# One-head layer: one score operation from two table columns, denominators of dense tiles on TensorE, dense means on ScalarE

## The chip, the core and the metric

The kernel runs on one core of one Trainium2 chip. The metric is the device time of one execution in microseconds (us), the median of several runs. The engines are TensorE (PE in the profile, its weight loads PEld), VectorE (DVE), ScalarE (ACT), GpSimd (POOL) and SyncE (SP), which here only issues transfers.

## What is computed

The reference is a stack of four graph attention layers on 3327 nodes with 512 features, all fp32. The adjacency is sparse (about 0.5% of its entries, the diagonal included). The layers have 8, 4, 1 and 8 heads. The change touches the third one alone, the layer with one head:

```python
h = features @ W
s1 = h @ attn[:512, 0]
s2 = h @ attn[512:, 0]
e = jax.nn.leaky_relu(s1[:, None] + s2[None, :], negative_slope=0.2)
e = jnp.where(adjacency > 0, e, -9e15)
h_prime = jax.nn.softmax(e, axis=1) @ h
return jax.nn.elu(h_prime)
```

Around it, as around every layer: `h = max(layernorm(x), 0)`, then `x = x + layer(h)`.

## The kernel before

**Tiles and order.** The nodes are ranked by their number of neighbours and cut into 26 tiles of 128 targets. For most tiles the neighbours' rows are gathered from a table in device memory by GpSimd's indirect transfers (`gather`, L835), one neighbour slot of all 128 targets at a time. In the one-head layer tiles 9 to 25 are done this way, and tiles 0 to 8, which have the most neighbours, are done densely over all 26 source blocks, with masks.

**The table.** A row has 528 columns: 256 features, 8 columns for scores, 256 features, 8 columns for scores. The score columns come out of the projection for free, because the products of the weights with the attention vectors are appended to the weights (class `Weights`, `fold`). In the one-head layer only the first of each 8 is used: column 256 holds a node's score as a target, column 520 (`ROW - 8`) its score as a source. The others are zero. One extra row, for empty slots, holds -30000 in all of the last 8 columns.

**Gathered tiles** (class `Tile`). The neighbours of a tile are taken in groups of up to four slots; a group is a step of the schedule, and the 17 tiles make 72 steps. `scored` copies the tile's own score once (L886), adds it to the neighbours' scores (L888), applies the slope 0.2 with a maximum (L890), and lets ScalarE take the exponential (L891). `group` accumulates weight times feature row on VectorE (L910, L912). When a tile is complete, `divisors` and `means` divide (L930 to L938), and `ends` places the rest: ELU, the addition to x, the next layer's normalization, transposes (L451), projection (L469) and the store of the next table (L996).

**Dense tiles** (class `Wholes`). They come in three groups of three tiles (384 targets). For each source block j, ScalarE computes r (`weights`, L1128), VectorE adds and masks it (`masked`, L1135, the tile em), and TensorE multiplies em with the block's feature rows into three banks, one for each tile (`products`, L1162). The denominators are column sums of em. GpSimd adds two blocks (`paired`, L1148), VectorE reduces two such pair sums and the sum so far (`added`, L1154), and at the end of the group TensorE sums over the partitions (`divisors`, L1169). VectorE then takes the reciprocal (L1173) and multiplies the three banks by it (`Whole.means`, L1089).

**Who goes when.** The order on VectorE, ScalarE, GpSimd and TensorE is written out by hand. A loop runs over the steps s and emits for each one: the gathers of step s + 4, the pieces hung at (s, "first"), the scores of step s + 1, the pieces at (s, "scored"), the accumulation of step s, and the pieces at (s, "last"). `later(s, place, piece)` hangs a piece in. Each engine then works through its own list in order. Dense block j of group p is masked at step 21p + floor(19j/26). Its products are emitted one step later, ahead of that step's mask product. The pair sum comes one step after its second block.

**Buffers.** The pool "o" holds one PSUM bank for the accumulator of a gathered tile and one for r. The pool "w" has three banks for the products, "t" has one for transposes, and the projection uses two. Gathered groups have five buffers, em has three pairs, and feature blocks of the dense part have four.

Of the kernel before, what the change touches and what calls it, by code (L numbers as in the profile page):

```python
# [10 lines left out]
F32 = mybir.dt.float32  # L11
# [4 lines left out]
OP = mybir.AluOpType  # L16
# [364 lines left out]
class Weights:  # L381
# [31 lines left out]

def centred(nc, xt, small, work):
# [382 lines left out]
def tile_gat_lists(ctx: ExitStack, tc: tile.TileContext, x, adj, ws, avs, out, ident, half, slots, L, low, spare, tabx, tabs):  # L797
# [48 lines left out]
    class Tile:  # L846
# [29 lines left out]
        def scored(self, i):  # L876

            H = HEADS[self.l]
            t = self.t
            k0, n, g = self.groups[i]  # L880
            if i == 0:
                self.po = pools["o"].tile([P, BANK], F32, name="bank")
                pw = next(scores)
                K = CAPS[t]
                self.wt, self.s = pw[:, :K * 8].rearrange("p (k h) -> p k h", h=8), pw[:, K * 8:K * 8 + H]
                nc.vector.tensor_copy(self.s, g[:, n, F:F + H] if self.l == 0 else g[:, 0, F // 2:F // 2 + H])  # L886
            z = small.tile([P, GROUP, 8], F32, name="z")[:, :n, :H]
            nc.vector.tensor_tensor(z, g[:, :n, ROW - 8:ROW - 8 + H],  # L888
                                    self.s.unsqueeze(1).to_broadcast([P, n, H]), OP.add)
# [37 lines left out]
        def divisors(self):  # L927
            H, K = HEADS[self.l], CAPS[self.t]
            den = self.den = small.tile([P, 8], F32, name="den")
            nc.vector.tensor_reduce(den[:, :H], self.wt[:, :K, :H].rearrange("p k h -> p h k"), AX.X, OP.add)  # L930
            nc.vector.tensor_scalar_max(den[:, :H], den[:, :H], TINY)
            nc.vector.reciprocal(den[:, :H], den[:, :H])
# [151 lines left out]
    class Whole(Tile):  # L1084


        def means(self):
            self.y = low[:, self.t % 3 * F:(self.t % 3 + 1) * F]
            nc.vector.tensor_scalar(self.y, self.po, self.den, None, OP.mult)  # L1089

    class Wholes:


        def __init__(self, l, W):
            self.l, self.tiles = l, [Whole(l, t, W) for t in range(ND)]
            self.s = pools["e"].tile([P, ND], F32, name="s", bufs=1)
            for t in range(ND):
                nc.sync.dma_start(self.s[:, t:t + 1], tabs[l % 2][t * P:(t + 1) * P, F // 2:F // 2 + 1])
            self.b, self.c, self.mc = [pools["e"].tile([P, NT], F32, name=n, bufs=1) for n in ("b", "c", "mc")]

            self.a = [low[:, 5 * F + p % 2 * wide:5 * F + (p % 2 + 1) * wide] for p in range(ND // 3)]
            self.v, self.e, self.mk, self.r, self.pairs, self.parts = {}, {}, {}, {}, {}, {}

        def targets(self, p):

# [12 lines left out]
        def weights(self, p, j):  # L1118
            if p == ND // 3:
                return  # L1120
            b, c, mc = [t[:, j:j + 1] for t in (self.b, self.c, self.mc)]
            if p == 0:
                d = self.v[p, j][:, ROW - 8:ROW - 7]
                nc.scalar.activation(b, d, AF.Exp)
                nc.scalar.activation(c, d, AF.Exp, scale=SLOPE)
                nc.scalar.activation(mc, c, AF.Copy, scale=-1.0)
            r = self.r[p, j] = pools["o"].tile([P, wide], F32, name="r")
            nc.scalar.activation(r, self.a[p], AF.Relu, scale=b, bias=mc)  # L1128

        def masked(self, p, j):  # L1130

            if j % 2 == 0:
                self.two = pools["e"].tile([P, 2, wide], F32, name="em", bufs=3)
            self.e[p, j] = self.two[:, j % 2, :]
            nc.vector.scalar_tensor_tensor(self.e[p, j], self.r.pop((p, j)), self.c[:, j:j + 1],  # L1135
                                           self.mk.pop((p, j)), OP.add, OP.mult)
            if j % 2:
                self.pairs[p, j // 2] = self.two

        def part(self, p, i):  # L1140
            if (p, i) not in self.parts:
                self.parts[p, i] = pools["e"].tile([P, 3, wide], F32, name="parts", bufs=2)
            return self.parts[p, i]

        def paired(self, p, i):

            two = self.pairs.pop((p, i))
            nc.gpsimd.tensor_tensor(self.part(p, i // 2)[:, 1 + i % 2, :], two[:, 0, :], two[:, 1, :], OP.add)  # L1148

        def added(self, p, i):  # L1150

            parts = self.part(p, i // 2)[:, i < 2:2 + i % 2, :]
            out_ = self.a[p] if i == NT // 2 - 1 else self.part(p, i // 2 + 1)[:, 0, :]
            nc.vector.tensor_reduce(out_, parts.rearrange("p j c -> p c j"), AX.X, OP.add)  # L1154

        def products(self, p, j):
            e, v = self.e.pop((p, j)), self.v.pop((p, j))
# [8 lines left out]
        def divisors(self, p):  # L1166
            self.pd = pools["t"].tile([P, F // P, P], F32, name="pt")
            for q in range(3):
                nc.tensor.matmul(self.pd[:, 0, q:q + 1], self.a[p][:, q * P:(q + 1) * P], one, start=True, stop=True)  # L1169
# [311 lines left out]
```

## Time and profile before

| | us |
|---|---|
| median of 3 runs | 2940.11 (2933.88 to 2944.69) |
| the profiled execution, its own time | 2959.5 |
| span of the profile | 2957.8 |
| busy in the span: TensorE | 2224.7 (75%) |
| VectorE | 1914.3 (65%) |
| GpSimd | 1728.5 (58%) |
| ScalarE | 931.8 (32%) |

A row of a group in the profile gives line, engine, operation, written and read tiles, shapes, count, then the busy time in us and the mean of one in ns, then the idle time of the engine just before it and what ended it. A row of waits gives total us, times, and the longest. "issue" means that the engine waited for nothing that the profile shows. A row of the timeline begins with the start and the duration in us; the bracket at its end is the idle time before it. One fp32 matmul shows as two instructions. Names ending in q are queues.

### The profile page before, as it was taken

The page shows a single profiled execution, that of the slowest core. Times are in us where ns is not written, and L with a number is a line of the kernel's source. Part 1 is how long each engine was busy: PE and PEld are TensorE (multiplying, and loading weights), DVE is VectorE, ACT ScalarE, POOL GpSimd, SP SyncE. Part 2 cuts the span into 40 slices and gives each one's busy share as a digit, 9 for nine tenths or more (in the row PEclk, how much of TensorE's full clock was granted, in tenths as well). Part 3 has the DMA queues.
Part 4 walks back from the last instruction along what each step waited for, and adds up shares of the span by engine and source line. Part 5 has one row for each costly group of instructions (what it writes and reads, how often), then busy time and mean ns, then how long its engine had stood idle before and what let it go on. Part 6 is the DMA issues. An engine that isn't in the chain of part 4 may idle for free.

```text
span 2957.8 us, 27080 instructions
## 1 busy us (share of the span) xinstructions
PE 2224.7 (75%) x7082; PEld 1251.4 (42%) x7082; DVE 1914.3 (65%) x4968; ACT 931.8 (32%) x2502; POOL 1728.5 (58%) x1717
## 2 busy tenths in 40 slices
PE   4777677787677745788877787689696778877887
PEld 2664243343333323344434344245354445444453
DVE  7887656565546523767765565698887556666665
ACT  5882122222221101323332222344333333333330
POOL 7894465565556663555655552676764555555554
PEclk9988788888888877899988889799897889988898
DMA  6885477677666675666766663788775666666664
GB/s 229 322 294 160 140 218 216 193 235 222 188 205 195 189 194 170 181 202 192 209 193 189 192 192 111 226 264 257 236 248 152 191 177 184 185 182 194 185 187 137
DMA packets 260730, 594.20 MB, mean 201 GB/s; under 512 B 103699, under 2 KB 121107, under 8 KB 256214
## 3 DMA queue, kind: packets, MB, share of 16 engines
q0 software_dynamic: 124368, 432.13, 49.8%
q1 hardware_dynamic: 132454, 153.45, 16.5%
q10 hardware_dynamic: 3744, 6.82, 0.7%
q8 instruction: 57, 0.93, 0.1%
q14 instruction: 107, 0.88, 0.1%
HBM read 542.60 MB, written 49.65 MB: 200 GB/s over the span
## 4 chain that ended last, share of the span: by engine, by line
DVE 21%; PE 18%; issue 16%; another core or an unknown queue 11%; ACT 6%; POOL 4%; DMA 3%; DVEq 0%; ACTq 0%; POOLq 0%; SPq 0%
PE bank L924 11%; DVE m L919 9%; POOL g L835 3%; PE pv L469 3%; PE whole L1310 3%; DVE bank L912 2%; DMA g<-tab,idxb 1%; DVE z L890 1%; DVE z L888 1%; ACT r L1276 1%; DVE x L962 1%; DVE q L439 1%; ACT pw L891 1%; DVE room L1292 1%
## 5 line engine op out<-in xcount | busy, mean ns | idle before, releaser
L924 PE MATMUL bank<-m,ident 128*128 128x512 f32 x2414 | 1236.5, 659 | 268.9 <-DVE m L919 137.5
L835 POOL DMA_INDIRECT g<-tab,idxb x712 | 678.2, 952 | 465.5 <-issue 189.3
L919 DVE TENSOR_TENSOR m<-g,pw 128x512 f32<-128x512 f32 x1207 | 752.0, 682 | 267.6 <-ACT pw L891 193.5
L924 PEld LDWEIGHTS bank<-m,ident 128*128 128x128 f32 x2414 | 490.2, 211 | 879.8 <-issue 568.9
L469 PE MATMUL pv<-w,hT 128*128 128x264 f32 x1664 | 447.4, 423 | 107.0 <-ACT hT L458 71.2
L835 POOL DMA_INDIRECT g<-tabx,twiceb x342 | 324.1, 948 | 245.8 <-issue 124.4
L835 POOL DMA_INDIRECT g<-tab,idxa x297 | 283.1, 953 | 262.1 <-DMA tab<-v 88.5
L469 PEld LDWEIGHTS pv<-w,hT 128*128 128x128 f32 x1664 | 339.5, 208 | 215.2 <-ACT hT L458 79.6
L891 ACT ACTIVATE pw<-z 128x32 f32<-128x32 f32 (+4 forms) x356 | 67.8, 190 | 945.4 <-DVE z L890 509.8
L1162 PE MATMUL whole<-ve,em 128*128 128x512 f32 x468 | 224.5, 632 | 48.2 <-DVE em L1135 27.9
L1310 PE MATMUL whole<-L,room 128*128 128x130 f32 x1248 | 171.1, 288 | 79.2 <-issue 79.0
L1310 PEld LDWEIGHTS whole<-L,room 128*128 128x128 f32 x1248 | 163.1, 201 | 107.1 <-issue 104.7
L695 POOL TENSOR_TENSOR key<-a,keys 128x3328 int32<-128x3328 int32 (+1 forms) x29 | 189.5, 6539 | 15.9 <-DVE cand L704 12.6
L912 DVE SCALAR_TENSOR_TENSOR bank<-g,L,bank 128x512 f32<-128x512 f32 x243 | 183.3, 754 | 9.9 <-remote 2.0
L835 POOL DMA_INDIRECT g<-tabx,twicea x99 | 94.4, 954 | 119.6 <-issue 75.3
L1162 PEld LDWEIGHTS whole<-ve,em 128*128 128x128 f32 x468 | 92.8, 203 | 158.7 <-issue 114.6
L451 PE MATMUL pt<-ident,xn 128*128 128x128 f32 x416 | 74.5, 302 | 93.0 <-issue 32.2
L704 DVE MAX8 cand<-key 128x8 f32<-128x208 int32 x416 | 143.6, 363 | 0.1
L890 DVE SCALAR_TENSOR_TENSOR z<-z 128x32 f32<-128x32 f32 (+5 forms) x428 | 82.5, 193 | 91.4 <-remote 61.4
L919 DVE TENSOR_TENSOR bank<-g,pw 128x512 f32<-128x512 f32 x74 | 51.5, 696 | 126.7 <-ACT pw L891 105.6
L1276 ACT ACTIVATE r<-low,L 128x384 f32<-128x384 f32 x208 | 121.2, 582 | 9.8 <-remote 3.9
L888 DVE TENSOR_TENSOR z<-g,pw 128x32 f32<-128x32 f32 (+4 forms) x356 | 61.8, 174 | 94.9 <-DMA g<-tab,idxa 39.0
(181 smaller groups left out, 2154.4 us busy)
## 6 DMA issues: line engine op xcount, KB each, us to landing
a<-in_adj SPq DMA_DIRECT2D x25, 1664.0 KB
tab<-v SPq DMA_DIRECT2D x78, 264.0 KB
ve<-tab SPq DMA_DIRECT2D x78, 264.0 KB
g<-tab SPq DMA_DIRECT2D x65, 264.0 KB
tabx<-vx SPq DMA_DIRECT2D x26, 528.0 KB
g<-tab,idxb POOLq DMA_INDIRECT x712
low<-tab SPq DMA_DIRECT2D x52, 132.0 KB
spare<-tab SPq DMA_DIRECT2D x52, 132.0 KB
```

The lines of the kernel that those rows point to most:

```text
L469: nc.tensor.matmul(pv[:, s, :HF + 8], hT[:, k, :], W.w[:, k, s, :], start=(k == 0), stop=(k == KC - 1))
L695: nc.gpsimd.tensor_tensor(key[:, c:c + quarter], a[:, c:c + quarter], keys[:, c:c + quarter], OP.mult)
L704: nc.vector.max(cand[:, g * 8:(g + 1) * 8], key[:, g * SEG:(g + 1) * SEG])
L835: nc.gpsimd.indirect_dma_start(out=out_, out_offset=None, in_=table, in_offset=bass.IndirectOffsetOnAxis(ap=which, axis=0))
L890: nc.vector.scalar_tensor_tensor(z, z, SLOPE, z, OP.mult, OP.max)
L891: nc.scalar.activation(self.wt[:, k0:k0 + n, :H], z, AF.Exp)
L912: nc.vector.scalar_tensor_tensor(acc, v, w, acc, OP.mult, OP.add)
L919: nc.vector.tensor_tensor(out_.rearrange("p (s h d) -> p s h d", s=2, d=D), v.rearrange("p s (h d) -> p s h d", d=D), wt[:, k0 + q, :H].re ...
L924: nc.tensor.matmul(self.po, ident, m[:, q, :], start=False, stop=(k0 + q == K - 1), skip_group_check=True)
L1162: nc.tensor.matmul(tl.po.rearrange("p (s m) -> p s m", s=2), e[:, q * P:(q + 1) * P], v.rearrange("p (s m) -> p s m", s=2)[:, :, :F // 2], ...
L1276: nc.scalar.activation(self.r[:, h, :], self.a[:, g, :], AF.Relu, bias=-1.0, scale=self.b[:, j, g:g + 1])
L1310: nc.tensor.matmul(dst, e[:, h, q * P:(q + 1) * P], mov, start=False, stop=(j == NT - 1), skip_group_check=True)
```

## The change

It has three parts, all in the one-head layer. First, the appended weight columns hold a second column each: the first one times 0.8 for the target's score, and times 0.2 for the source's. The table then holds 0.8 of a node's target score in column 257 and 0.2 of its source score in column 521. With s the target's and d the source's score, the step takes max(d + 0.8s, 0.2d) in one VectorE operation, and ScalarE copies 0.8s once for a tile. Second, each pair sum goes straight to TensorE, which adds its column sums to three columns for each group of tiles (`added`). These columns lie in the same PSUM bank as r, which is now one fixed tile. The step of `added` is s + 3, "first", for every pair; `divisors` and the partial sums are gone. Third, the means of dense tiles are ScalarE copies with a scale. Nothing changes in the transfers.

```diff
@@ Weights.fold
+        if self.H == 1:
+            nc.vector.tensor_scalar(self.w[:, k, s, HF + 1:HF + 2], self.w[:, k, s, HF:HF + 1],
+                                    SLOPE if s else 1.0 - SLOPE, None, OP.mult)
@@ Tile.scored
-                nc.vector.tensor_copy(self.s, g[:, n, F:F + H] if self.l == 0 else g[:, 0, F // 2:F // 2 + H])
+                if H == 1:
+                    nc.scalar.activation(self.s, g[:, 0, F // 2 + 1:F // 2 + 2], AF.Copy)
+                else:
+                    nc.vector.tensor_copy(self.s, g[:, n, F:F + H] if self.l == 0 else g[:, 0, F // 2:F // 2 + H])
             z = small.tile([P, GROUP, 8], F32, name="z")[:, :n, :H]
+            if H == 1:
+                nc.vector.scalar_tensor_tensor(z, g[:, :n, ROW - 8:ROW - 7], self.s, g[:, :n, ROW - 7:ROW - 6],
+                                               OP.add, OP.max)
+                nc.scalar.activation(self.wt[:, k0:k0 + n, :H], z, AF.Exp)
+                return
@@ Whole.means
-            nc.vector.tensor_scalar(self.y, self.po, self.den, None, OP.mult)
+            nc.scalar.activation(self.y, self.po, AF.Copy, scale=self.den)
@@ Wholes.__init__
+            bank = pools["o"].tile([P, BANK], F32, name="r")
+            self.r, self.pd = bank[:, :wide], [bank[:, wide + 8 * p:wide + 8 * p + 3] for p in range(ND // 3)]
@@ Wholes.weights
-            r = self.r[p, j] = pools["o"].tile([P, wide], F32, name="r")
-            nc.scalar.activation(r, self.a[p], AF.Relu, scale=b, bias=mc)
+            nc.scalar.activation(self.r, self.a[p], AF.Relu, scale=b, bias=mc)
@@ Wholes.paired
-            nc.gpsimd.tensor_tensor(self.part(p, i // 2)[:, 1 + i % 2, :], two[:, 0, :], two[:, 1, :], OP.add)
+            self.sums[p, i] = pools["e"].tile([P, wide], F32, name="sums", bufs=3)
+            nc.gpsimd.tensor_tensor(self.sums[p, i], two[:, 0, :], two[:, 1, :], OP.add)
@@ Wholes.added
-            parts = self.part(p, i // 2)[:, i < 2:2 + i % 2, :]
-            out_ = self.a[p] if i == NT // 2 - 1 else self.part(p, i // 2 + 1)[:, 0, :]
-            nc.vector.tensor_reduce(out_, parts.rearrange("p j c -> p c j"), AX.X, OP.add)
+            both = self.sums.pop((p, i))
+            for q in range(3):
+                nc.tensor.matmul(self.pd[p][:, q:q + 1], both[:, q * P:(q + 1) * P], one, start=(i == 0 and q == 0),
+                                 stop=(i == NT // 2 - 1), skip_group_check=True)
@@ Wholes.divisors
-            self.pd = pools["t"].tile([P, F // P, P], F32, name="pt")
-            for q in range(3):
-                nc.tensor.matmul(self.pd[:, 0, q:q + 1], self.a[p][:, q * P:(q + 1) * P], one, start=True, stop=True)
@@ Wholes.means
-            nc.vector.reciprocal(den, self.pd[:, 0, :3])
+            nc.vector.reciprocal(den, self.pd[p])
@@ Wholes.place
                         later(s + 1, "first", lambda p=p, i=i: self.paired(p, i))
-                        if i % 2 or j == NT - 1:
-                            later(s + 2, "last", lambda p=p, i=i: self.added(p, i))
-                later(s + 3, "first", lambda p=p: self.divisors(p))
+                        later(s + 3, "first", lambda p=p, i=i: self.added(p, i))
                 later(s + 3, "last", lambda p=p: self.means(p))
```

More of the change, by code (lines that the diff above doesn't have):

```diff
@@ L1101, in __init__ @@
             self.a = [low[:, 5 * F + p % 2 * wide:5 * F + (p % 2 + 1) * wide] for p in range(ND // 3)]
-            self.v, self.e, self.mk, self.r, self.pairs, self.parts = {}, {}, {}, {}, {}, {}
+            self.v, self.e, self.mk, self.pairs, self.sums = {}, {}, {}, {}, {}
+            bank = pools["o"].tile([P, BANK], F32, name="r")
+            self.r, self.pd = bank[:, :wide], [bank[:, wide + 8 * p:wide + 8 * p + 3] for p in range(ND // 3)]
         def targets(self, p):
@@ L1134, in masked @@
             self.e[p, j] = self.two[:, j % 2, :]
-            nc.vector.scalar_tensor_tensor(self.e[p, j], self.r.pop((p, j)), self.c[:, j:j + 1],
+            nc.vector.scalar_tensor_tensor(self.e[p, j], self.r, self.c[:, j:j + 1],
                                            self.mk.pop((p, j)), OP.add, OP.mult)
@@ L1138, in masked @@
                 self.pairs[p, j // 2] = self.two
[L1140 to L1143, printed above, removed]
         def paired(self, p, i):
             two = self.pairs.pop((p, i))
-            nc.gpsimd.tensor_tensor(self.part(p, i // 2)[:, 1 + i % 2, :], two[:, 0, :], two[:, 1, :], OP.add)
+            self.sums[p, i] = pools["e"].tile([P, wide], F32, name="sums", bufs=3)
+            nc.gpsimd.tensor_tensor(self.sums[p, i], two[:, 0, :], two[:, 1, :], OP.add)
         def added(self, p, i):
-            parts = self.part(p, i // 2)[:, i < 2:2 + i % 2, :]
-            out_ = self.a[p] if i == NT // 2 - 1 else self.part(p, i // 2 + 1)[:, 0, :]
-            nc.vector.tensor_reduce(out_, parts.rearrange("p j c -> p c j"), AX.X, OP.add)
+            both = self.sums.pop((p, i))
+            for q in range(3):
+                nc.tensor.matmul(self.pd[p][:, q:q + 1], both[:, q * P:(q + 1) * P], one, start=(i == 0 and q == 0),
+                                 stop=(i == NT // 2 - 1), skip_group_check=True)
         def products(self, p, j):
@@ L1164, in products @@
                                  start=(j == 0), stop=(j == NT - 1))
-        def divisors(self, p):
-            self.pd = pools["t"].tile([P, F // P, P], F32, name="pt")
-            for q in range(3):
-                nc.tensor.matmul(self.pd[:, 0, q:q + 1], self.a[p][:, q * P:(q + 1) * P], one, start=True, stop=True)
         def means(self, p):
             den = small.tile([P, 3], F32, name="den3")
-            nc.vector.reciprocal(den, self.pd[:, 0, :3])
+            nc.vector.reciprocal(den, self.pd[p])
             for q in range(3):
```

## The prediction

> **What bounds the kernel now.** I read the granted clock first (0.867, one core), then stretches of time, to find the layer that the change touches, then groups by shape, waits and the timeline inside it. The one-head layer runs from about 1845 to 2285 us. Layer 3's gathers cannot start before its table is stored, so what is saved here comes off the whole. Busy time by stretch:
>
> ```profile
> core 0: us, PE busy (x) PEld busy (x) DVE busy (x) ACT busy (x) POOL busy (x), PEclk, DMA share, GB/s
> 1845.00:1890.00 45.00, 20.46 (x46) 8.94 (x44) 18.96 (x38) 11.06 (x37) 31.54 (x34) 0.76 0.76 236
> 1890.00:2235.00 345.00, 290.49 (x856) 160.74 (x856) 298.25 (x599) 138.02 (x329) 235.20 (x249) 0.92 0.80 244
> 2235.00:2295.00 60.00, 37.17 (x130) 28.43 (x131) 41.69 (x94) 22.93 (x50) 23.67 (x27) 0.76 0.44 134
> ```
>
> In the middle 345 us VectorE is busy 298, TensorE 290, ScalarE only 138. GpSimd shows 235, but each gather is followed by a gap without any wait (first line below): with these 48 us it is occupied 283. So three engines lie within a fifth of each other. Who waits for whom there:
>
> ```profile
> POOL g L835 <- issue: 48.2, 171, 0.3
> POOL root L431 <- DVE ve L978: 30.4, 11, 8.3
> POOL g L835 <- DVE bank L912: 13.1, 9, 3.4
> ACT r L1128 <- DVE em L1135: 75.2, 36, 5.5
> PE whole L1162 <- DVE em L1135: 27.9, 9, 12.6
> DVE em L1135 <- issue: 9.3, 8, 4.0
> ```
>
> GpSimd, ScalarE and TensorE all wait for VectorE; VectorE's own listed waits add up to 34.5 us. It is the leader, with TensorE close behind. The groups that the change touches (whole layer):
>
> ```profile
> L1128 ACT ACTIVATE r<-low,mc,b 128x384 f32<-128x384 f32 x78 | 52.6, 674 | 139.6 <-DVE em L1135 75.2 <-issue 31.7 <-DVE z L888 9.4
> L1154 DVE TENSOR_REDUCE parts<-parts 128x384 f32<-128x1152 f32 x15 | 22.0, 1467 | 0.0
> L888 DVE TENSOR_TENSOR z<-g,L 128x4 f32<-128x4 f32 x58 | 14.1, 243 | 16.2 <-DMA g<-tab,idxa 14.7 <-issue 0.9
> L1089 DVE TENSOR_SCALAR low<-whole,den 128x512 f32<-128x512 f32 x9 | 6.2, 744 | 0.1
> L886 DVE COPY L<-g 128x1 f32<-128x1 f32 x16 | 2.3, 144 | 0.0
> ```
>
> And five rows of the timeline, from different moments:
>
> ```profile
> 2037.07 0.62 DVE L1135 SCALAR_TENSOR_TENSOR em<-r,c,mk 128x384 f32<-128x384 f32 x1 [4.00 <-issue]
> 2071.01 2.00 DVE L956 SCALAR_TENSOR_TENSOR low<-ex,low 128x512 f32<-128x512 f32 x1
> 2071.44 1.01 POOL L1148 TENSOR_TENSOR parts<-em 128x384 f32<-128x384 f32 x1
> 2112.34 0.80 PE L1169 MATMUL pt<-one,low 128*128 128x1 f32 x6 [2.90 <-DVE den L930]
> 2119.58 2.93 PE L1162 MATMUL whole<-ve,em 128*128 128x512 f32 x3 [6.43 <-DVE low L1089]
> ```
>
> **Two rules of the Trainium skill.** "PSUM — Partial Sum Buffer", section "PSUM bank collisions raise a hardware error": two engines must not be in one bank at once, also at different columns, so a shared bank has to be passed on by waits. The trace shows that passing for two engines, where r is written by ScalarE and read by VectorE (75.2 us of ScalarE waiting, 36 times). The change puts the denominators of TensorE into that bank, so a third engine joins. The built program agrees: 35 of the 78 mask products (L1135) now wait for the last denominator matmul, issued just before them; before, 32 waited for TensorE, but for products some steps old. For the price I go by the trace, since the page gives none. "SBUF — State Buffer", section "Who interferes with whom": a VectorE operation with two SBUF inputs contends with a GpSimd instruction that reads SBUF. The trace agrees: L956 takes 0.69 us, and 2.00 us across the pair sum at 2071.44; of the 72 L888, 11 that overlap a pair sum average 0.62 us, the other 61 0.16. The remaining score operation still reads two SBUF operands, so I leave that stretching in.
>
> **Part by part, in the 345 us.**
>
> 1. Reductions of partial sums leave VectorE: 20 of 21 fall here. 22.0 us, 2.9 (three of the short shape) and two of the three final ones at 0.96: −26.8 us.
> 2. Dense means to ScalarE: six of nine here, 6 x 0.744 = −4.5 us. ScalarE does a 128x528 copy out of PSUM in 0.69 us (L476), so it gains 4.2 us beside 138 busy of 345: no cost while it has this room. Without it, the next group's first product is late, which waits for these banks.
> 3. One score operation instead of two: from start to start L888 takes 0.20 us; about 59 groups: −11.8 us.
> 4. The copy of a tile's own score goes to ScalarE: 14 x 0.144 = −2.0 us. But VectorE's score now waits for ScalarE, whose queue holds the next r in front of it (r starts when the mask product ends). At a tile's first group that is up to 0.67 + 0.19 us, or 12 us in 14 tiles; 3 us if ScalarE is free. I take +10.
> 5. Denominators on TensorE: 39 sums of three fp32 matmuls, two instructions each, as L1169 has them. Six took 0.80 us warm, at 0.11 us from start to start, so 0.67 us in a stream; after a pause 1.41 us. 37 fall here: +25 us, less 2 us for two removed sets of L1169. That lies on TensorE alone.
> 6. The new wait. Ahead of the denominators in TensorE's queue stand the products and, in many steps, a projection of 3.7 us. I compared the start of each mask product concerned with the time at which TensorE had finished what stands ahead (35 places, the group ends left out). TensorE was ready in 25, by 0.4 to 21 us, and late in 10, in four clusters whose worst values are 0.8, 6.9, 5.0 and 0.5 us: 13 us, about half of it waited for already by another way (VectorE's 4.00 us at 2037.07 is r standing behind a ScalarE copy that waits for TensorE). So +6, and 10 x 0.67 = +7 where TensorE is the late one. Behind the waiting product in VectorE's queue stand the scores and accumulations, and behind those GpSimd's buffers and roots. The pair sum itself ended 2 us or more ahead in all these places after the start of the layer.
> 7. At a group's end the chain loses a reduction: pair sum, matmuls, reciprocal, means. TensorE's 6.43 us at 2119.58 shrinks by about 1 us at two ends; left out.
>
> VectorE: −45.1 + 10 + 13 = −22, so 323 us. TensorE: 290.5 + 23, and at the two group ends some 13 us that it must still wait: 326 us. GpSimd: 283 and its waits. So the stretch comes to about 326, −19 us. Behind it, until 2278, VectorE loses another reduction (0.96), three means (2.2) and 13 score operations (2.6), in part given back to the last gathers: −3 us. Before it the loads of tables set the pace: 0. In layer 0 eight small operations prepare the columns, 0.15 us each by L964's duration: +1 us. In sum −21 us.
>
> The profiled execution took 2959.5 us (span 2957.8 and 1.7 around it): 2938 after. It lies 19 us above the median of 2940.1, with nothing in this layer that explains it, so the same step from the median: **2919 us**.
>
> **Rivals.**
>
> *The hand-off decides (slower).* Every second mask product waits for TensorE's queue, and TensorE, idle more often, runs its slow pitch. The relief on VectorE is 35 us net of step 4. Thirty-five hand-offs eat it at 1.0 us each, and the kernel is slower by 0.5% from 1.45 us each. At 1.5 to 1.6 us it gives some 2958. For it: a projection of 3.7 us often stands ahead, 6.7 us in the slow pitch at 1985. Against: TensorE was ready in 25 of 35.
>
> *TensorE takes over (same).* Its 313 busy us pack no better than now (290 in 345), and the relief disappears in it: about 2936. For it: TensorE leads already in the four clusters.
>
> *Full relief (faster).* The waits for ScalarE and TensorE hide, GpSimd's 44 us of waiting for VectorE (two rows above) shrink with them. VectorE alone would allow −45, but GpSimd at 283 and TensorE with its pauses stop the stretch near 305: −40, and −3 behind it, about 2897.
>
> *It doesn't do what it says.* The score's slope identity holds: max(s+d, 0.2(s+d)) is 0.2s + max(0.8s+d, 0.2d), and the factor of 0.2s cancels in a row's softmax. Padding rows hold the same large negative number in both columns. I give it nothing.
>
> **How the numbers follow.** 0.5%, about 15 us, is what a measurement of this kernel can tell from no change. Forecast 0.35, full relief 0.18, TensorE takes over 0.27, hand-off 0.20. The forecast's own spread reaches past 2925 a little; so faster 0.50, same 0.28, slower 0.22. The likeliest case alone holds 2908 to 2930. For the range I go from 2893, just past full relief, to 2956, where most of the hand-off's case is taken in.
>
> **What would show it.** In the after profile the reductions and L888 are gone for this layer, and VectorE's busy time falls by about 50 us. Step 4: a wait of the score for ScalarE's copy, under 1 us each, some 16 of them. Step 6: the mask product waiting for TensorE, 13 us in sum; 40 or more means the hand-off's rival. Step 5: 234 matmul instructions with one column at 0.11 us. The one-head layer should take 418 us instead of 440. I am wrong if it is unchanged with TensorE waiting as much as now, or if another layer moves by more than 5 us.

## The result and the profile after

The changed kernel takes 2962.07 us (median of 20 runs, 2944.28 to 2986.33) against 2941.4 us before (median of 20). The ratio is 1.0073, 95% interval 1.0048 to 1.0097. So it is slower by 0.5 to 1.0%, where 2919 us had been forecast. (Ratios, here and below, leave out runs more than 1.5% above the fastest of the same kernel, so a few lie above the quotient of the medians.)

The one-head layer, from its first gather to the first gather of the next layer, takes 469.4 us in the profile after and 447.0 us in the one before: +22.4 us. (These 447.0 us are the prediction's 440, counted from first gather to first gather.) The medians differ by 20.7 us. The profiled execution itself took 2953.57 us, less than the 2959.5 us of the one profiled before: layer 1 began at 1134 us instead of 1145, and layer 3 took 653 us instead of 661. The change touches neither of them, and they vary by 10 us from run to run. So from here on only the one-head layer is compared.

Line numbers have moved by 3 to 14: the score operation is L896, the mask product L1149, r is L1142, the products L1173, the means L1101, the projection L472. L1164 are the denominator matmuls. Busy time in the whole span, then in the stretches of the layer that answer to those of before (the middle one ends with the last steps of the dense part):

```profile
PE 2228.2 (75%) x7298; PEld 1267.7 (43%) x7298; DVE 1874.3 (63%) x4857; ACT 940.9 (32%) x2528; POOL 1731.4 (59%) x1717
```
```profile
core 0: us, PE busy (x) PEld busy (x) DVE busy (x) ACT busy (x) POOL busy (x), PEclk, DMA share, GB/s
1826.00:1871.00 45.00, 21.35 (x45) 9.88 (x44) 15.89 (x28) 10.33 (x38) 28.50 (x30) 0.74 0.73 229
1871.00:2237.00 366.00, 319.11 (x1072) 186.60 (x1070) 266.04 (x512) 147.24 (x355) 240.18 (x252) 0.93 0.76 232
2237.00:2299.00 62.00, 40.16 (x146) 30.52 (x146) 34.84 (x74) 23.78 (x52) 24.54 (x28) 0.78 0.41 125
```

VectorE did get lighter: 266 us in the middle stretch instead of 298, and 317 instead of 359 in the whole layer. The stretch grew by 21 us all the same, from 345 to 366. TensorE has 319 us in it instead of 290. It is now the engine with the most work, and it idles for 47 us instead of 55: of its additional 29 us, 21 came on top of the time. The groups by shape (whole layer) say where VectorE went, first the mask product in the profile before, then four rows of the profile after:

```profile
L1135 DVE SCALAR_TENSOR_TENSOR em<-r,c,mk 128x384 f32<-128x384 f32 x78 | 47.8, 612 | 24.8 <-issue 10.1 <-ACT r L1128 8.5 <-ACT hT L458 4.8
```
```profile
L1173 PE MATMUL whole<-ve,em 128*128 128x512 f32 x468 | 232.7, 646 | 19.5 <-issue 7.8 <-ACT low L1101 6.8 <-DVE em L1149 4.9
...
L1149 DVE SCALAR_TENSOR_TENSOR em<-r,c,mk 128x384 f32<-128x384 f32 x78 | 47.9, 615 | 72.8 <-PE r L1164 20.9 <-remote 16.6 <-issue 10.7
...
L1164 PE MATMUL r<-one,sums 128*128 128x1 f32 x234 | 32.7, 255 | 38.4 <-ACT L L898 13.6 <-issue 11.7 <-ACT r L1142 8.1
L896 DVE SCALAR_TENSOR_TENSOR z<-g,L 128x4 f32<-128x4 f32 x58 | 20.5, 353 | 39.9 <-DMA g<-tab,idxa 21.1 <-ACT L L890 11.7 <-issue 3.3
```

The second number behind the second bar is what counts. The mask product idles for 72.8 us before it starts, where it was 24.8 us: +48 us, more than all that VectorE was relieved of. The score idles for 11.7 us for ScalarE's copy by this list. And the products, which waited 27.9 us for the mask product before, now wait 4.9 us for it: TensorE hardly waits for the mask product any more, the mask product waits for TensorE. The rows of waits in the middle stretch:

```profile
DVE em L1149 <- PE r L1164: 20.9, 7, 8.9
DVE z L896 <- ACT L L890: 11.7, 5, 6.5
DVE em L1149 <- remote: 7.4, 1, 7.4
ACT r L1142 <- DVE em L1149: 88.3, 43, 8.6
```

At the tiles' first groups I read the timeline one by one: 13 scores wait for the copy, 19.4 us in sum, ten of them for 0.87 to 0.93 us, which is one r and the copy itself on ScalarE, and three for 1.5, 2.6 and 6.5 us.

The releaser named in a row is an inference ("remote" is one that the profile could not place, on a kernel of one core), so I read the hand-offs one by one. At each of the 35 mask products that wait for a denominator matmul, TensorE's lateness is the time from when VectorE and r were both ready to the end of the last matmul waited for. It is 32.9 us in sum, in 14 of the 35 places. The largest one in the timeline (start, duration, then what ran; rows of other engines left out):

```profile
2009.85 5.40 PE L1173 MATMUL whole<-ve,em 128*128 128x512 f32 x12
...
2013.79 0.61 DVE L1149 SCALAR_TENSOR_TENSOR em<-r,c,mk 128x384 f32<-128x384 f32 x1
...
2014.44 3.12 DVE L924 SCALAR_TENSOR_TENSOR bank<-g,L,bank 128x512 f32<-128x512 f32 x4
...
2015.52 3.73 PE L472 MATMUL pv<-w,hT 128*128 128x264 f32 x16
...
2019.08 2.74 PE L1173 MATMUL whole<-ve,em 128*128 128x512 f32 x6
...
2022.09 3.73 PE L472 MATMUL pv<-w,hT 128*128 128x264 f32 x16
...
2025.66 0.72 PE L1164 MATMUL r<-one,sums 128*128 128x1 f32 x6
...
2026.47 0.62 DVE L1149 SCALAR_TENSOR_TENSOR em<-r,c,mk 128x384 f32<-128x384 f32 x1 [8.91 <-PE r L1164]
2027.13 0.68 ACT L1142 ACTIVATE r<-low,mc,b 128x384 f32<-128x384 f32 x1 [4.24 <-DVE em L1149]
```

VectorE is done at 2017.56 and stands still for 8.91 us. TensorE meanwhile works almost without a pause through the rest of a projection, products and a second projection; then come 0.72 us of denominators, and 0.09 us after their end the mask product starts. The pair sum for them had been ready since 2014.24. What costs the time is not the 0.72 us of the matmuls but their place behind two projections in TensorE's queue, and behind VectorE's wait ScalarE's next r waits as well.

### The profile page after: what moved, and what is told of

It reads as the page before. It is cut to its first block, busy times and chain, and to the rows that moved or that the text cites. A ratio compares the mean times of both kernels' runs of the same rounds, so it can differ in the third digit from the quotient of the medians.

```text
span 2951.8 us, 27533 instructions
## 1 busy us (share of the span) xinstructions
PE 2228.2 (75%) x7298; PEld 1267.7 (43%) x7298; DVE 1874.3 (63%) x4857; ACT 940.9 (32%) x2528; POOL 1731.4 (59%) x1717
## 4 chain that ended last, share of the span: by engine, by line
DVE 18%; issue 16%; PE 16%; another core or an unknown queue 8%; ACT 6%; POOL 4%; DMA 3%; DVEq 0%; SPq 0%; POOLq 0%; ACTq 0%
DVE m L931 8%; PE bank L936 8%; POOL g L838 3%; PE pv L472 3%; PE whole L1173 3%; ACT r L1280 2%; PE whole L1314 1%; DVE bank L924 1%; DVE room L1296 1%; DMA g<-tab,idxb 1%; DVE q L442 1%; ACT L L1291 1%; DVE x L974 1%; DVE z L902 1%
## 5 line engine op out<-in xcount | busy, mean ns | idle before, releaser
L936 PE MATMUL bank<-m,ident 128*128 128x512 f32 x2414 | 1214.7, 649 | 272.6 <-DVE m L931 150.6
L936 PEld LDWEIGHTS bank<-m,ident 128*128 128x128 f32 x2414 | 480.3, 207 | 874.1 <-issue 559.6
L472 PE MATMUL pv<-w,hT 128*128 128x264 f32 x1664 | 444.9, 422 | 119.3 <-ACT hT L461 80.7
L472 PEld LDWEIGHTS pv<-w,hT 128*128 128x128 f32 x1664 | 339.1, 208 | 225.1 <-ACT hT L461 88.4
L1173 PE MATMUL whole<-ve,em 128*128 128x512 f32 x468 | 232.7, 646 | 19.5 <-issue 7.8
L1173 PEld LDWEIGHTS whole<-ve,em 128*128 128x128 f32 x468 | 92.8, 206 | 120.6 <-issue 104.3
L479 ACT ACTIVATE v<-pv,root 128x528 f32<-128x528 f32 x78 | 53.8, 690 | 186.0 <-remote 92.9
```

The source lines that it names most:

```text
L472: nc.tensor.matmul(pv[:, s, :HF + 8], hT[:, k, :], W.w[:, k, s, :], start=(k == 0), stop=(k == KC - 1))
L936: nc.tensor.matmul(self.po, ident, m[:, q, :], start=False, stop=(k0 + q == K - 1), skip_group_check=True)
L1173: nc.tensor.matmul(tl.po.rearrange("p (s m) -> p s m", s=2), e[:, q * P:(q + 1) * P], v.rearrange("p (s m) -> p s m", s=2)[:, :, :F // 2], ...
```

## The experiments

The runs came in four groups; all kernels, the one before too, were at 2940 us in the first (x), 2440 us in the second and third (z, c) and 2920 us in the fourth (d), so each is compared with before of its own group. "Layer" is the one-head layer of the profile; "idle" is the idle time before all mask products.

| run | median, us | ratio to before [95%] | layer, us | idle, us |
|---|---|---|---|---|
| before (x) | 2939.11 | | 447.0 | 24.8 |
| changed kernel | 2962.07 | 1.0073 [1.0048, 1.0097] | 469.4 | 72.8 |
| x1_r_sbuf | 2942.26 | 1.0054 [1.0028, 1.0080] | 444.6 | 31.1 |
| x2_dens_as_before | 2935.41 | 1.0016 [0.9992, 1.0040] | 447.2 | 25.1 |
| x3_dens_alone | 2967.20 | 1.0140 [1.0084, 1.0195] | 473.9 | 79.0 |
| x4_copy_dve | 2956.28 | 1.0110 [1.0050, 1.0171] | 457.4 | 78.3 |
| z1_batch | 2441.54 | 1.0003 [0.9990, 1.0016] | 432.6 | 49.1 |
| z2_r_sbuf_direct | 2426.95 | 0.9946 [0.9933, 0.9960] | 415.9 | 33.6 |
| y2_parts13_direct | 2426.53 | 0.9952 [0.9936, 0.9968] | 417.1 | 26.6 |
| z4_score_direct | 2437.78 | 0.9988 [0.9979, 0.9996] | 427.6 | 27.7 |
| c_before | 2441.32 | | 429.4 | 26.6 |
| c_after | 2450.51 | 1.0031 [1.0014, 1.0048] | 443.8 | 59.7 |
| c_batch | 2444.19 | 1.0011 [1.0000, 1.0021] | 431.1 | 47.2 |
| c_r_sbuf_two | 2423.85 | 0.9926 [0.9911, 0.9942] | 408.9 | 25.4 |
| d_before | 2920.97 | | 443.2 | 25.5 |
| d_both | 2955.26 | 1.0107 [1.0064, 1.0150] | 470.6 | 62.1 |
| d_r_sbuf_two | 2907.51 | 0.9950 [0.9926, 0.9974] | 426.7 | 22.6 |

The changed kernel's row is the result above, against its own 2941.4 us. The x and z groups had no profile of the kernel before: for x the first one (447.0) stands in, for z c_before, at the same level. Each layer and idle time is that of one profiled execution; before itself gave 447.0 and 443.2 us at nearly one level, so a difference of some 4 us says little. In the x group runs of one kernel spread over 2%, and ratio and quotient of the medians differ (1.0054 and 1.0011 for x1), so there I lean on the layers.

### Which part costs

**x1_r_sbuf**: the changed kernel with r in SBUF, so that the denominators have the bank to themselves and no mask product waits for them.

```diff
-            self.r, self.pd = bank[:, :wide], [bank[...] for p in range(ND // 3)]
+            self.r = pools["e"].tile([P, wide], F32, name="rs", bufs=1)
+            self.pd = [bank[...] for p in range(ND // 3)]
```

> The changed kernel with one difference: r lies in SBUF (one buffer, as before), so the denominator columns have their PSUM bank to themselves and no mask product waits for a denominator matmul. Theory (the hand-off of the shared bank costs what the change lost): the mask product's wait for TensorE falls from some 48 us to under 15, the one-head layer falls from 469 to 430 us or less, the kernel to 2915 to 2930. Rival (the matmuls themselves load TensorE too much, wherever their sums lie): the layer stays at 460 to 470 us and the kernel at 2955 to 2965, with TensorE as busy as now. A cost of its own: the mask product then reads two SBUF operands and can be stretched by pair sums.

**x2_dens_as_before**: the score operation and the dense means as changed, the denominators as before.

```diff
-            for q in range(3):
-                nc.tensor.matmul(self.pd[p][:, q:q + 1], both[:, q * P:(q + 1) * P], one, start=(i == 0 and q == 0),
-                                 stop=(i == NT // 2 - 1), skip_group_check=True)
+            nc.vector.tensor_reduce(out_, parts.rearrange("p j c -> p c j"), AX.X, OP.add)
...
```

and with it the partial sums, the divisors and the r of before.

> The score operation from two columns with ScalarE's copy and the dense means on ScalarE as in the changed kernel; the denominators as before, by VectorE. Theory (the denominators are the whole loss): the layer is 435 to 445 us, 2 to 12 below before, the kernel 2928 to 2940; VectorE loses 20 us of work and waits 12 for ScalarE's copies. Rival (the copies or the means on ScalarE bring the loss): layer above 455, kernel above 2950.

**x3_dens_alone**: the reverse, the kernel before with only its denominators changed.

```diff
-            nc.vector.tensor_reduce(out_, parts.rearrange("p j c -> p c j"), AX.X, OP.add)
+            for q in range(3):
+                nc.tensor.matmul(self.pd[p][:, q:q + 1], both[:, q * P:(q + 1) * P], one, start=(i == 0 and q == 0),
+                                 stop=(i == NT // 2 - 1), skip_group_check=True)
...
```

> The kernel before with only the denominators moved to TensorE, in r's bank. Theory: all of the loss is here; VectorE sheds 28 us of reductions and gets the hand-offs, the layer is 465 to 475 us, the kernel 2958 to 2970. Rival (copies or means bring the loss): layer 440 or less, kernel 2935 or less.

**x4_copy_dve**: the changed kernel with the copy of a tile's own score on VectorE again.

```diff
-                    nc.scalar.activation(self.s, g[:, 0, F // 2 + 1:F // 2 + 2], AF.Copy)
+                    nc.vector.tensor_copy(self.s, g[:, 0, F // 2 + 1:F // 2 + 2])
```

> The changed kernel with the copy of a tile's own score on VectorE again (17 operations of 0.14 us); nothing else. If the wait of the score for ScalarE's copy, 12 us in the changed kernel's trace, lies on the path, the layer falls by 6 to 10 us and the kernel to 2952 to 2956. If the hand-off swallows what VectorE gains, the layer stays within 3 us of 469 and the mask product's wait for TensorE grows by as much as the other wait shrinks.

The loss sits in the denominators. With them alone (x3) the layer takes 26.9 us more than before; without them (x2) 0.2 us more. And it sits in their bank: with the same 234 matmuls on TensorE, but r elsewhere (x1), the layer is 2.4 us shorter than before. Two forecasts were missed all the same: x1's layer was to fall to 430 us or less and its time to 2915 to 2930 us, and x2's layer was to be 2 to 12 us below before. Groups by shape, the mask product in x3 and in x1:

```profile
L1137 DVE SCALAR_TENSOR_TENSOR em<-r,c,mk 128x384 f32<-128x384 f32 x78 | 48.0, 615 | 79.0 <-PE r L1152 30.2 <-remote 21.0 <-ACT r L1130 10.3
```
```profile
L1150 DVE SCALAR_TENSOR_TENSOR em<-rs,c,mk 128x384 f32<-128x384 f32 x78 | 61.4, 787 | 31.1 <-issue 20.2 <-ACT rs L1143 6.1 <-POOL root L434 4.0
```

In x1 the idle time is nearly back at 24.8 us, but the mask product itself is 787 ns long instead of 615. That is a price of its own: it now reads r and the mask from SBUF, and 15 of the 78, those that overlap a pair sum of GpSimd, average 1496 ns; the other 63 average 619. The Trainium skill's "SBUF — State Buffer", section "Who interferes with whom", says that a VectorE operation with two SBUF inputs contends with a GpSimd instruction that reads SBUF. This trace agrees, at some 880 ns more for each of the 15.

x4 takes 12.0 us less in the layer than the changed kernel, although it puts the copy's 2.3 us back on VectorE: the waits for ScalarE's copy cost about that much. (The time of the whole kernel does not show it: the ratios to before are 1.0110 and 1.0073, with intervals that overlap. y2 below supports it.) The idle time before the full-size score groups falls from 39.9 us to 17.9. Their group in x4:

```profile
L896 DVE SCALAR_TENSOR_TENSOR z<-g,L 128x4 f32<-128x4 f32 x58 | 24.6, 424 | 17.9 <-DMA g<-tab,idxa 14.8 <-DMA g<-tab,idxb 1.8 <-issue 0.5
```

No wait for a copy is left in this row; what remains of it, 14.8 us, is the wait for gathers that the kernel before has too.

### How the cost grows with the number of hand-offs

**z1_batch**: the same matmuls, issued for four, four and five pair sums at a time. Only 8 mask products then wait for a denominator matmul just issued, instead of 35.

```diff
-                        later(s + 3, "first", lambda p=p, i=i: self.added(p, i))
+                        if i in (3, 7, NT // 2 - 1):
+                            k = {3: 0, 7: 4}.get(i, 8)
+                            later(s + 3, "first", lambda p=p, i=i, k=k: [self.added(p, m) for m in range(k, i + 1)])
```

with seven buffers for the pair sums instead of three.

> Changed kernel with the same 234 denominator matmuls on TensorE in r's bank, but issued in batches of four, four and five pair sums, so that 8 mask products instead of 35 wait for a denominator matmul just issued. Hand-off theory (1.37 us each in the changed kernel): a hand-off behind a batch of 12 to 15 matmuls is longer, about 3 us, so some 25 us instead of 48: the mask product's idle time falls from 72.8 us to 45-55, the layer from 469 us to 440-452, the kernel to about 2940. Rival, TensorE's 32 us of extra work decide and not the places at which it is waited for: the layer stays at 463-470, the kernel at 2955-2962.

At the level of 2440 us this could not be set against the changed kernel, so both ran again with a profile of before beside them:

> The kernel before once more, for its profile beside the three others of this call (the second group of runs had a chip on which all kernels take about 2440 us instead of 2940, so layers are to be compared within one chip). On that chip both theories expect a one-head layer of 428-434 us, with some 25 us of idle time before the mask products.

> The changed kernel once more, beside the others of this call. Hand-off theory: the same 35 waits cost here too, the mask product's idle time is 65-80 us, the layer 15-25 us longer than that of the kernel before, the kernel 0.6 to 1.0% slower. Rival, the loss of the first result came from that chip's slower memory or from layers that the change leaves alone: layer within 5 us of before.

> The kernel with batches (8 hand-offs instead of 35) once more, so that it stands beside the changed kernel on one chip. Hand-off theory: layer 15-25 us shorter than the changed kernel's and about that of the kernel before; idle time of the mask product 45-55 us. Rival, TensorE's extra work decides: layer as the changed kernel's, within 5 us.

The mask product in the three:

```profile
L1135 DVE SCALAR_TENSOR_TENSOR em<-r,c,mk 128x384 f32<-128x384 f32 x78 | 47.7, 612 | 26.6 <-ACT r L1128 26.6
```
```profile
L1149 DVE SCALAR_TENSOR_TENSOR em<-r,c,mk 128x384 f32<-128x384 f32 x78 | 47.9, 615 | 59.7 <-PE r L1164 29.7 <-ACT r L1142 19.4 <-ACT hT L461 7.7
```
```profile
L1149 DVE SCALAR_TENSOR_TENSOR em<-r,c,mk 128x384 f32<-128x384 f32 x78 | 47.8, 613 | 47.2 <-PE r L1164 27.2 <-ACT r L1142 14.3 <-issue 2.5
```

Here the changed kernel loses less: 14.4 us in the layer and 0.31%, below the 15 to 25 us and 0.6 to 1.0% that I had expected. TensorE's lateness at the hand-offs is about the same, 36.0 us in 17 of the 35 places. The batches win 12.7 of the 14.4 us back (15 to 25 had been expected), with the same work on TensorE, 373 us busy in the layer. So the number of places decides, not the work. But the cost does not go down in proportion: the 8 hand-offs that are left hold 6 waits of 27.2 us in sum. At the same two mask products the wait grew from 8.9 us (c_after) to 11.9 and from 4.9 to 8.3, and a batch of twelve takes 2.7 us there where a set of three took 0.7.

### Whether the slack was misread or used up

**d_both**: the kernel before with the new denominators, and with the reductions left on VectorE too, their result unused. VectorE keeps its old work, and the same 35 mask products wait.

```diff
+                        if i % 2 or j == NT - 1:
+                            later(s + 2, "last", lambda p=p, i=i: self.reduced(p, i))
                         later(s + 3, "first", lambda p=p, i=i: self.added(p, i))
```

> The kernel before, for its profile on the chip of this call: one-head layer 428-450 us depending on the chip, 25 us of idle time before the mask products.

> The kernel before, with the denominator matmuls on TensorE in r's bank added, and the reductions of partial sums left on VectorE as well (their result is not used). So VectorE keeps its old work and arrives at the mask products as late as before, and the same 35 of them wait for a denominator matmul. Theory A (the slack of step 6 was read at VectorE's old pace, and the relief itself uses it up): here TensorE is the late one in about 10 of the 35 places, 13 us in sum, and the layer is 8-18 us longer than before. Theory B (the reading of the slack was wrong in itself, since TensorE's queue moves too): TensorE is late by 30 us or more in sum as in the changed kernel (33 us in 14 places), and the layer is 25 us longer or more.

```profile
L1138 DVE SCALAR_TENSOR_TENSOR em<-r,c,mk 128x384 f32<-128x384 f32 x78 | 47.9, 614 | 62.1 <-issue 20.7 <-remote 18.3 <-ACT r L1131 11.3
```

TensorE is late by 25.3 us in 13 of the 35 places, and the layer is 27.4 us longer than d_before's. So theory A is wrong: even at VectorE's old pace it is twice the forecast's 13 us, and the layer grows by as much. Theory B holds for the layer; its 30 us of lateness are not quite reached.

The relief is used up as well. x3 is the same kernel without the reductions on VectorE: 335 us busy in the layer instead of 358. Its layer is 26.9 us over the first profile of before, d_both's 27.4 over d_before's, so removing 23 us of VectorE work was worth 0.5 us, which is nothing within the scatter of the profiles. The mask product's idle time is 79.0 us instead of 62.1, and TensorE's lateness 42.0 us instead of 25.3: most of what VectorE no longer computes, it waits.

### What the other parts are worth

**y2_parts13_direct**: x2 (denominators as before) with the first score of a tile reading the own score from the gathered row, so that no score waits for the copy.

```diff
-                nc.vector.scalar_tensor_tensor(z, g[:, :n, ROW - 8:ROW - 7], self.s, g[:, :n, ROW - 7:ROW - 6],
+                own = g[:, 0, F // 2 + 1:F // 2 + 2] if i == 0 else self.s
+                nc.vector.scalar_tensor_tensor(z, g[:, :n, ROW - 8:ROW - 7], own, g[:, :n, ROW - 7:ROW - 6],
```

> Denominators as before the change (reductions on VectorE); one score operation and dense means on ScalarE kept; first score operation of a tile reads the own score directly. Theory: the wait for the copy, 15 us in the run without this edit, was what ate the relief of VectorE: layer 435-440 us against 447, kernel about 2929. Rival, the wait covers time that VectorE would have waited elsewhere (GpSimd's gathers, TensorE's products): layer 445-448, kernel 2935-2940.

**z4_score_direct**: y2 with the dense means on VectorE.

```diff
-            nc.scalar.activation(self.y, self.po, AF.Copy, scale=self.den)
+            nc.vector.tensor_scalar(self.y, self.po, self.den, None, OP.mult)
```

> As the run with denominators as before and the direct first score, but with the dense means on VectorE again, so that only the score operation is changed from the kernel before. Theory: dense means cost VectorE 6.7 us in the layer (nine of 744 ns) and are worth up to that: layer 3-7 us longer than in the run with means on ScalarE. Rival, the means lie where VectorE has nothing to do or delay the next group's r on ScalarE: no difference, within 2 us, or shorter.

y2 is 12.3 us shorter in the layer than c_before, and 0.48% faster: the wait for the copy was real. The split is a surprise. The score operation alone (z4) gives 1.8 us and 0.12%, the dense means 10.5 us in the layer, 8.8 by the two ratios (0.36% of 2440 us), where they cost VectorE 6.2 us. The intervals of the two ratios leave some 4 us either way, so the means are worth about their length; whether they are worth more, and why, no run shows.

The score operation gives little because the one that is left is dearer. The two of before in c_before, and the one in c_after:

```profile
L890 DVE SCALAR_TENSOR_TENSOR z<-z 128x4 f32<-128x4 f32 x58 | 12.7, 220 | 2.0
L888 DVE TENSOR_TENSOR z<-g,L 128x4 f32<-128x4 f32 x58 | 12.7, 218 | 16.1 <-DMA g<-tab,idxa 15.5
```
```profile
L896 DVE SCALAR_TENSOR_TENSOR z<-g,L 128x4 f32<-128x4 f32 x58 | 20.3, 349 | 38.1 <-DMA g<-tab,idxa 18.9 <-ACT L L890 16.7 <-DMA g<-tab,idxb 2.3
```

Two of 218 and 220 ns became one of 349. Over all 72 groups, clear of GpSimd's compute, they take 159 and 168 ns, and the new one 222; the 20 of the new ones that overlap it average 587 ns (before, 17 at 369 and 14 at 378).

### A version that keeps the relief

**z2_r_sbuf_direct**: x1 and the direct first score together. **c_r_sbuf_two**, and the same again as **d_r_sbuf_two**: r in two SBUF buffers besides.

```diff
+            self.r = pools["e"].tile([P, wide], F32, name="rs", bufs=2)
             nc.scalar.activation(self.r, self.a[p], AF.Relu, scale=b, bias=mc)
```

> Changed kernel with r in SBUF (no hand-off with TensorE) and with the first score operation of a tile reading the own score from the gathered rows directly, so that it does not wait for ScalarE's copy. Theory: both new waits are gone and what is left is the relief of VectorE less the stretched mask product (787 ns instead of 615): layer 432-438 us against 447 before and 444.6 with r in SBUF alone, kernel about 2931. Rival, TensorE (380 us busy in the layer) is the bound by now and takes the gain: layer 443-446, kernel as with r in SBUF alone, about 2940.

> Changed kernel with r in two SBUF buffers instead of one and the direct first score: ScalarE can write the next r while VectorE reads this one, so that the mask product waits neither for TensorE nor for ScalarE. Theory: of its 33 us of idle time with one buffer some 15 to 20 are waits for r; layer 5-12 us shorter than the 416 us with one buffer on the faster chip, kernel about 0.8% faster than before. Rival, TensorE or GpSimd is the bound by then (TensorE 359 us busy, GpSimd 298 us beside its pauses): layer within 3 us of that with one buffer, kernel 0.5% faster than before.

> The changed kernel with r in two SBUF buffers and the direct first score once more, on the chip of this call: 0.6 to 0.9% faster than before if what it gained (0.74%) does not hang on one chip; within 0.3% if it does.

With one buffer the layer takes 415.9 us, shorter than I had expected on the scale of 447, because the level was lower; against 429.4 it is 13.5 us less, and the time 0.54% less. The second buffer brings the layer to 408.9 us, 20.5 us less than c_before, and the kernel to 0.74% less [0.58, 0.89]. At the level of 2920 us it is 16.5 us and 0.50% [0.26, 0.74], a little under the 0.6 to 0.9% expected. It beats both kernels. Of the 20.5 us, y2 has 12.3 without any denominators on TensorE, so the move of the denominators itself is worth some 8 us here, and with one buffer (z2) next to nothing. The whole layer in windows of its own, c_before, c_after and c_r_sbuf_two (columns as in the table of stretches):

```profile
1506.10:1935.40 429.30, 345.01 (x1034) 197.15 (x1034) 357.29 (x730) 170.55 (x415) 290.14 (x308) 0.90 0.77 239
```
```profile
1505.50:1949.30 443.80, 373.90 (x1258) 222.96 (x1258) 315.88 (x612) 181.22 (x443) 292.79 (x309) 0.91 0.76 231
```
```profile
1502.10:1911.10 409.00, 357.58 (x1250) 218.59 (x1250) 321.05 (x612) 178.34 (x441) 302.49 (x309) 0.93 0.81 251
```

VectorE's work in the last two differs by 5 us and GpSimd's by 10 (TensorE's 16 us less have a higher granted clock beside them, 0.93 instead of 0.91), but their time differs by 35. VectorE's idle time before the mask products falls from 59.7 to 25.4 us. 9 us of that are given back in the mask products themselves, 740 ns each instead of 615.

## Why the prediction was wrong, step by step

**Step 6, the new wait, failed.** It was put at 13 us; the lateness measured is 32.9 us, and the layer pays 27 us for the hand-off alone (d_both). The direction, the 35 places and nine of the ten late ones were right. What was wrong is the count. In the trace of before, TensorE was behind at ten places, by 0.75, 0.51, 0.57, 6.94, 3.97, then 4.97, 3.04, 4.21, 1.08 and 0.50 us. I took the worst of each cluster, as if one wait would bring VectorE and TensorE into step for the rest of it. The sum over all ten is 26.5 us, and 33 with 0.67 us of denominators for each. Measured, the denominators included, are 25.3 us in d_both and 32.9 in the changed kernel. A wait does shorten the next one of its cluster, but does not remove it: the places that were behind by 6.94 and 3.97 us are late by 8.8 and 1.8 in the trace after, and those behind by 4.97 and 3.04 are late by 6.0 and 1.2. At the second place of both pairs a projection stands directly in front of the denominators. Halving the 13 us because "about half of it" was waited for already was the second mistake: in d_both the mask product's idle time grew by 36.6 us, more than TensorE's lateness, so nothing of it was covered by the waits of before.

**The sum failed with it.** The length of the stretch was taken as the longer of two: VectorE's 323 us, which are the 345 of before less its relief, and TensorE's 326, which are 313 of work and 13 of waiting at two group ends. Measured are 319 us of work on TensorE and 47 of idle time, in 366. And the relief of VectorE did not count: x3 and d_both show that under the hand-off 23 us of it are worth 0.5 us. Before, TensorE waited for the mask product, and the mask product waited for TensorE, in the listed waits, only by way of ScalarE (4.8 us behind hT); now it waits for TensorE directly, and saved work turns into such waiting. That the stretch as a whole follows TensorE's queue is not shown: a removed wait for ScalarE was worth 12 us under the same hand-off (x4). The pieces, 27.4 us for the hand-off (d_both), 0.2 for the other two parts with the copy's wait (x2) and −0.5 for the reductions, come to 27, where 22.4 were measured; the difference is no larger than that between two profiles of before.

**Step 1, the reductions**, left VectorE as forecast: in d_both they take 27.8 us, and VectorE is busy 23 us less without them. But their worth was lost.

**Step 2, the dense means**, was right or too low: 6.7 us in the layer by the two places of the prediction, 10.5 measured by the layers and 8.8, some 4 either way, by the ratios.

**Step 3, the score operation**, was too high. 72 groups at 0.20 us made 14.4 us; the group took 30.0 us before and 23.4 us after (c_before, c_after, all shapes), so 6.6 us. The removed operation was costed at its own pitch, and the one that stays at its old length; it reads two strided columns and takes 222 ns instead of 168, and 587 where it overlaps GpSimd's compute. The layer gained 1.8 us by it (z4).

**Step 4, the copy**, was close: −2 and +10 us forecast, and x4, which undoes both, gains 12.0 us where 8 were expected. Ten of the 13 waits have the forecast's price, 0.67 + 0.19 us. Left out were the three longer ones: at the largest, 6.5 us, ScalarE's queue holds not only an r ahead of the copy but also the small exponentials for that block and the exponential of the next group's target row, which waits for TensorE.

**Step 5, TensorE's work**, was a little low: 32.7 us in all where 0.67 us by 39 makes 26. A set of three took 0.84 us in the mean, 0.72 right behind other work and up to 1.44 after a pause.

**The rivals.** The hand-off's rival was right in its direction: 48 us of additional idle time over 35 places is 1.37 us each, between its break-even of 1.0 and the 1.45 from which it counted on 0.5%. That its 2958 us come so near to 2962 is in part luck. Not every second mask product waits, but 14 of 35 for TensorE, 32.9 us, under the 40 that were to be its sign; and the slow pitch that it gave as a reason shows in 6 of the 39 sets of denominators only (1.16 to 1.44 us), and TensorE idles less than before, not more. It had a chance of 0.20, held down by "TensorE was ready in 25 of 35", which was true (21 in the trace after) and beside the point, since the 14 late ones are late by 2.35 us in the mean, and four of them by 2.7 to 8.8 us. "TensorE takes over" is not what happened either: with the hand-off gone, the same matmuls fit into 409 us (358 busy, c_r_sbuf_two), closer than before (345 busy in 429), in part at a higher granted clock (0.93 instead of 0.90). "Full relief" did not come with the change. That c_r_sbuf_two gains 20.5 us and the forecast was 21 is a coincidence: it has no wait for the copy, which was put at 10 us, and a longer mask product instead, and at the level of 2920 us it gains 16.5. Step 7 was not tried apart.

## What to carry to other kernels

When a change puts a third engine's output into a bank that two others pass back and forth, price the wait by what stands ahead in the third engine's queue at every single hand-off, and add up all the late ones, the new work included (here 33 us, where 25 to 33 were measured); do not net them within a cluster or against waits that exist already. Under such a wait, work saved on the waiting engine may be worth nothing: 23 us of VectorE's were (x3, d_both), though a wait removed elsewhere on it was worth 12 us (x4). What brought the loss back was another buffer (r elsewhere: −24.8 us of layer, x1), or fewer hand-offs (8 instead of 35: −12.7 us). Two operations merged into one are not one removed; look for a row of the merged form, or bound it.

## What was not expected of the hardware

- The mask product is 612 ns with r in PSUM whatever GpSimd does (611 across a pair sum, 612 clear of it, in c_before), but with r in SBUF 1496 ns across one and 619 clear (x1). Moving an operand out of a contested bank so cost VectorE 13 us of work in the layer.
- The 234 one-column matmul instructions occupied TensorE for 32.7 us, 0.14 us each. The 468 product instructions with 512 columns took 232.7 us, 0.50 us each: a column count 512 times as large for 3.6 times the time.
- The level of all kernels changed between the groups of runs (2440 us is 17% under 2940), and on one chip between the third and the fourth (2440 and 2920); the DMA engines moved 201 GB/s over the span in the changed kernel's first profile and 244 GB/s in z1_batch's. Why was not tried. The loss by the change was smaller at the quicker level, 14.4 us of layer instead of 22.4, with TensorE as late as before (36.0 and 32.9 us).
